# Fifteen products of 64x64 blocks in place of eighteen: g, phi and theta of blocks 2 to 8 by one scheme

## The chip, the cores and the metric

The kernel runs on one core of one Trainium2 chip. Its metric is device time in microseconds (us) of one execution. The median of three runs of the kernel before is 2480.83 us (2480.46 to 2481.8).

## The reference, cut to what matters

x has 4 images of 128 channels and 96 x 96 pixels, all in float32. Two layers of the same form, with weights of their own, are applied to it one after the other:

```python
g_x     = maxpool2(conv1x1(x, g_w, g_b))       # 128 -> 64 channels, 48 x 48 = 2304 keys
theta_x = conv1x1(x, theta_w, theta_b)         # 128 -> 64 channels, 9216 queries
phi_x   = maxpool2(conv1x1(x, phi_w, phi_b))
f    = einsum('bqc,bck->bqk', theta_x, phi_x)
attn = softmax(f, axis=-1)
y    = einsum('bqk,bkc->bqc', attn, g_x)
x    = batchnorm(conv1x1(y, W_w, W_b)) + x
```

Image and layer make eight blocks of work. A 1x1 convolution is a matrix product over the channels: g, phi and theta are three 64 x 128 matrices that meet the same x.

## The kernel before, in words

`shifted_blocks` computes everything; `general_blocks` is a second form that runs only when a flag says that sums of exponentials left their limits.

**Blocks, pairs, steps.** The order of the eight blocks is `ORDER`, which alternates images so that a block's x is finished in time. A block has 9 pairs; a pair is 1024 queries. The 2304 keys are 18 tiles of 128, taken two at a time, so a pair takes 9 steps, and a cycle of 18 steps takes an even and an odd pair. All 648 steps are one loop over `t`; `s` is `t` modulo 18, and `q` is the even pair's number.

**A step on TensorE.** The array is used as four independent 64x64 tiles. A step issues the scores of its first key tile (four products of 64 x 64 by 512 columns, `scores`, line 607), then whatever extra group the step has (`first`), then the scores of the second tile, then a second extra (`second`), then the value products of the two tiles of the step before (`values`, line 629). I call four products side by side a group. ScalarE takes `exp` of each score tile from one of two PSUM buffers (`ps_sc`, line 612). VectorE adds up the exponentials (`add_up`, lines 619 and 621); `take`, the eviction of the extra group, stands between the two add_ups of a step, or behind them. After that come the steps that were put off with `later(t, ...)`.

**What hangs on fixed steps of a cycle.** `folds` turn and add the sums of exponentials by transfers (SP and POOL queues) and DVE's `turn` at s = 15 and s = 24; `normalise` at s = 1 and 11; the projection `multiply` (line 780) at s = 3 and 13, evicted by ScalarE and added to x by an adding transfer (`add`, line 795); `put` stores a finished pair of layer 2.

**Keys and values of the next block.** While a block's pairs run, units prepare the next block's g and phi (class `Unit`). The first block makes its own (`pooled`, `chunks`). A unit covers 1536 pixels, two groups of 768; six units make a block. Its four steps (`first` to `fourth`, `UNITS`) use seven products of 64x64 blocks where the plain form takes eight, with sums of x in `sums` made by plain and adding transfers (`build`, `BUILDS`, line 434), and combined weights in `mixed`. Each step fills the two banks of `ps_misc`, which thetas, W and units share. DVE combines the products in `stage` (lines 479 to 513), pools them (517), computes the centre of phi (`centring`, lines 528 and 529), and transposes g into `gT` (559). ScalarE writes phi minus the centre in two arrangements (`spread`, lines 545, 548 and 552). Of these, `pool(1)` and `centring` are put one step after `fourth`, and `spread` a step later (`AFTER`).

**Theta.** Thetas of two pairs are made by `thetas`: two groups of 512 columns in two steps that follow each other, at s = 5 and 6 (6 and 7 in the first cycle), evicted by ScalarE (line 601). The last pair's is made alone (`theta_alone`).

**The second layer's weights** are turned and combined by DVE and ScalarE in small pieces at s = 1 and 17 of the first cycles (`late_steps`).

Of the kernel before, what the change touches and what calls it, by code (L numbers as in the profile page):

```python
# [16 lines left out]
P = 128  # L17
# [20 lines left out]
UR = 16  # L38
NU = H // UR
UN = 4 * W  # L40
UK = UN // 4
UB = 2 * UK // 32
TB = NKT // 2
UNITS = ((15, 16, 18, 20), (25, 26, 28, 30))
BUILDS = ((10, 11, 12, 12, 15), (18, 19, 20, 20, 22))
STORE = 3
AFTER = ((1, 1, 2, 4, 5), (1, 2, 2, 3, 4))
THETAS = (6, 5)
# [5 lines left out]
NORM, PROJECT = (1, 11), (3, 13)  # L54
SQ = 32
# [9 lines left out]
def shifted_blocks(ctx: ExitStack, tc: tile.TileContext, x: bass.AP, layers, out: bass.AP, flag):  # L65
# [53 lines left out]
    stage = const.tile([P, NK], F32, name="stage")  # L119
    sums = [const.tile([P, 2, UN], F32, name=f"sums_{i}") for i in range(2)]  # L120
# [40 lines left out]
    class Layer:  # L161
# [40 lines left out]
        def steps_mixed(self):  # L202

            low, high = slice(0, CI), slice(CI, P)
            g, phi = slice(0, CI), slice(CI, 2 * CI)
            m = self.mixed = const.tile([P, 3, CI], F32, name=f"mixed_{self.l}")
            w = self.gphi

            def crossed():
                nc.scalar.copy(m[low, 1, :], w[high, phi])  # L210
                nc.scalar.copy(m[high, 2, :], w[low, g])
                nc.scalar.copy(m[high, 1, :], w[low, phi])

            def combined():
                nc.vector.tensor_sub(m[low, 0, :], w[low, phi], m[low, 1, :])
                nc.vector.tensor_sub(m[high, 0, :], m[high, 1, :], w[high, phi])
                nc.vector.tensor_sub(m[high, 0, :], m[high, 0, :], m[high, 2, :])
                nc.vector.tensor_sub(m[high, 1, :], m[high, 2, :], m[high, 1, :])
                nc.vector.tensor_add(m[high, 2, :], w[high, g], m[high, 0, :])

            def copied():
                nc.scalar.copy(m[low, 2, :], m[high, 0, :])

            return [crossed, combined, copied]
# [63 lines left out]
    class Block:  # L288
# [6 lines left out]
        def begin_keys(self):  # L295
            name = self.name
            self.phi = kvp.tile([P, NK], F32, tag="phi", name=f"phi_{name}")
            self.gT = kvp.tile([P, NKT, CI], F32, tag="gT", name=f"gT_{name}")
            self.centre = kvp.tile([P, 1], F32, tag="centre", name=f"centre_{name}")

# [114 lines left out]
    class Unit:  # L415


        def __init__(self, blk, u):
            self.blk, self.u, self.name = blk, u, f"{blk.name}_{u}"
            self.s = stage[:, : 4 * UN].rearrange("p (i n) -> p i n", i=4)  # L420
            self.keys = stage[:, 4 * UN : 4 * UN + 4 * UK]
            self.half = stage[:CI, 4 * UN + 4 * UK :].rearrange("p (c n) -> p c n", c=2)

        def pixels(self, i, rows):
            some = self.blk.xt[rows, ts(self.u, UR * W)]
            return some.rearrange("p (c i n) -> p c i n", c=2, i=2)[:, :, i, :]

        def build(self):

            low, high = slice(0, CI), slice(CI, P)  # L430
            one, two = sums

            def add(dst, src):
                nc.gpsimd.dma_start(out=dst, in_=src, accum_op=ALU.add)  # L434

            def load():
                nc.sync.dma_start(out=one, in_=self.pixels(0, slice(0, P)))
                nc.sync.dma_start(out=two[high], in_=self.pixels(1, low))
                nc.sync.dma_start(out=self.half, in_=self.pixels(1, low)[:, :, UN // 2 :])

            def load_rest():
                nc.sync.dma_start(out=two[low], in_=self.pixels(1, high))

            def add_one():
                add(one[high], self.pixels(0, low))
                add(one[low], self.pixels(1, low))

            def add_two():
                add(self.half, one[high, :, UN // 2 :])
                add(two[high], one[high])  # L450

            return load, add_one, load_rest, add_two, lambda: add(two[low], two[high])

        def both(self, *some):
            for c in range(2):
                for bank, lhsT, rhs in some:
                    nc.tensor.matmul(  # L457
                        bank[ts(c, CI), :UN], lhsT=lhsT, rhs=rhs[:, c, :], start=True, stop=True
                    )

# [7 lines left out]
        def first(self):  # L468
            self.pss = two_banks(f"unit_ps_{self.name}")
            self.A, self.B = (ps[:, :UN] for ps in self.pss)  # L470
            low, high, w = slice(0, CI), slice(CI, P), self.blk.w.gphi
            self.both(
                (self.pss[0], w[low, :CI], self.pixels(1, low)),
                (self.pss[1], w[high, :CI], self.pixels(1, high)),
# [3 lines left out]
        def first_sum(self):  # L478
            nc.vector.tensor_add(self.s[:, 1, :], self.s[:, 0, :], self.B)

        def second(self):
            self.part(self.blk.w.mixed[CI:, 0, :], sums[1][CI:, :, : UN // 2], 0)

        def second_rest(self):
            self.part(self.blk.w.mixed[:CI, 2, :], self.half, 1)

        def second_sum(self):
            for i in range(2):
                dst, cols = self.s[:, 0, ts(i, UN // 2)], ts(i, UN // 2)
                nc.vector.tensor_add(dst, dst, self.pss[i][:, cols])  # L490

        def third(self):
            m = self.blk.w.mixed
            self.both(
                (self.pss[0], m[CI:, 1, :], sums[0][CI:]),
                (self.pss[1], m[:CI, 0, :], sums[0][:CI]),
            )

        def third_sum(self):
            nc.vector.tensor_add(self.s[:, 3, :], self.s[:, 0, :], self.A)  # L500
            nc.vector.tensor_sub(self.s[:, 2, :], self.B, self.s[:, 3, :])
            nc.vector.tensor_sub(self.s[:, 0, :], self.B, self.s[:, 0, :])

        def fourth(self):
            m = self.blk.w.mixed
            self.both(
                (self.pss[0], m[:CI, 1, :], sums[1][:CI]),
                (self.pss[1], m[CI:, 2, :], self.pixels(0, slice(CI, P))),
            )

        def fourth_sum(self):
            nc.vector.tensor_add(self.s[:, 3, :], self.s[:, 3, :], self.A)
            nc.vector.tensor_add(self.s[:, 0, :], self.s[:, 0, :], self.B)

        def pool(self, i):

            nc.vector.tensor_reduce(  # L517
                self.keys[:, ts(i, 2 * UK)].rearrange("p (h w) -> p h w", w=W // 2),
                self.s[:, ts(i, 2), :].rearrange(
                    "p i (h a w b) -> p (i h) w a b", a=2, b=2, w=W // 2  # L520
                ),
# [3 lines left out]

        def centring(self):
            centre = self.blk.centre
            nc.vector.tensor_reduce(centre[:CI, :], self.keys[:CI, 2 * UK :], AX.X, ALU.add)
            nc.vector.tensor_scalar(
                centre[:CI, :], centre[:CI, :], -1.0 / (2 * UK), None, ALU.mult  # L530
            )

        def parts(self):

            b = self.u * UB
            while b < (self.u + 1) * UB:
                n = min((self.u + 1) * UB, (b // TB + 1) * TB) - b
                yield b - self.u * UB, n, b // TB, b % TB
                b += n

        def spread(self):
            src = self.keys[:, 2 * UK :].rearrange("p (b k) -> p b k", k=32)
            planes = self.blk.planes().rearrange("p i (t k) -> p i t k", k=KT)
            if self.u == 0:
                nc.scalar.copy(self.blk.centre[CI:, :], self.blk.centre[:CI, :])
            for m, n, k, t in self.parts():
                dst = planes[:, :, t : t + n, ts(k, 32)]
                nc.scalar.activation(
                    dst[:, 0], src[:, m : m + n, :], AF.Identity, bias=self.blk.centre
                )  # L550
                for h in range(2):
                    nc.scalar.copy(dst[ts(1 - h, CI), 1], dst[ts(h, CI), 0])

        def square(self, side):
            src = self.keys[ts(side, CI), : 2 * UK].rearrange("p (b k) -> p b k", k=32)
            for m, n, k, t in self.parts():
                t += side * TB
                for c in range(CI // 32):
                    nc.vector.transpose(  # L559
                        self.blk.gT[ts(k, 32), t : t + n, ts(c, 32)],  # L560
                        src[ts(c, 32), m : m + n, :],
                    )

    class Pair:
# [7 lines left out]

        def theta(self, ps):
            for h in range(2):
                nc.tensor.matmul(
                    ps[ts(h, CI), :], lhsT=self.blk.w.theta,
                    rhs=self.blk.xt[:, ts(2 * self.p + h, QT)], start=True, stop=True,
                )

        def theta_alone(self):  # L580

            pss = two_banks(f"theta_ps_{self.name}")

            def make():
                for c in range(2):
                    for r in range(2):
                        nc.tensor.matmul(
# [804 lines left out]
```

## Time and profile before

| | |
|---|---|
| median of 3 runs | 2480.83 us |
| the profiled execution | 2480.92 us, span 2479.1 us, granted clock 0.999 |
| PE busy | 2468.9 us (100%) |
| DVE busy | 1974.8 us (80%) |
| ACT busy | 1670.1 us (67%) |
| POOL busy | 660.6 us (27%) |
| DMA, mean | 99 GB/s, 245.27 MB |
| queue q0 (transfers issued by POOL) | 119.78 MB, 34.7% of 16 engines |
| queue q1 (issued by SP) | 121.66 MB, 17.5% |

The span runs from the first to the last instruction that the profiler recorded; the execution is 1.8 us longer. Busy is the union of an engine's instructions. PE is TensorE, PEld its weight loads, DVE VectorE, ACT ScalarE, POOL GpSimd and SP SyncE. A name such as L621 is a line of the kernel, and `sum<-sum,exp` says what is written and from what. In the timeline a row has start, length, engine, line, operation and a count, and in brackets the idle time before it and what ended it. In the list of waits a row has total us, number of waits and the longest.

### The profile page before, as it was taken

The page shows a single profiled execution, that of the slowest core. Times are in us where ns is not written, and L with a number is a line of the kernel's source. Part 1 is how long each engine was busy: PE and PEld are TensorE (multiplying, and loading weights), DVE is VectorE, ACT ScalarE, POOL GpSimd, SP SyncE. Part 2 cuts the span into 40 slices and gives each one's busy share as a digit, 9 for nine tenths or more (in the row PEclk, how much of TensorE's full clock was granted, in tenths as well). Part 3 has the DMA queues.
Part 4 walks back from the last instruction along what each step waited for, and adds up shares of the span by engine and source line. Part 5 has one row for each costly group of instructions (what it writes and reads, how often), then busy time and mean ns, then how long its engine had stood idle before and what let it go on. Part 6 is the DMA issues. An engine that isn't in the chain of part 4 may idle for free.

```text
span 2479.1 us, 57705 instructions
## 1 busy us (share of the span) xinstructions
PE 2468.9 (100%) x23391; PEld 1145.3 (46%) x23391; DVE 1974.8 (80%) x2458; ACT 1670.1 (67%) x1836; POOL 660.6 (27%) x776
## 2 busy tenths in 40 slices
PE   9999999999999999999999999999999999999998
PEld 5444444444444444444444444444444444444443
DVE  7888878887778887888777887788876888766777
ACT  6666666666666666766666676666666666666665
POOL 0333132322133322232222332322222223222210
PEclk9999999999999999999999999999999999999999
DMA  4666465643456736575345664655435556344433
GB/s 165 104 114 133 86 121 97 114 81 60 72 104 118 134 76 118 113 132 114 70 78 110 117 118 78 130 101 98 82 61 88 109 112 113 75 78 78 78 70 61
DMA packets 151170, 245.27 MB, mean 99 GB/s; under 512 B 30310, under 2 KB 92400, under 8 KB 150896
## 3 DMA queue, kind: packets, MB, share of 16 engines
q0 software_dynamic: 69664, 119.78, 34.7%
q1 hardware_dynamic: 81064, 121.66, 17.5%
q8 instruction: 185, 3.03, 0.5%
q14 instruction: 89, 0.73, 0.1%
q10 hardware_dynamic: 168, 0.07, 0.0%
HBM read 37.56 MB, written 19.16 MB: 23 GB/s over the span
## 4 chain that ended last, share of the span: by engine, by line
PE 98%; DVE 1%; DMA 0%; issue 0%; ACT 0%; SPq 0%; DVEq 0%; ACTq 0%
PE sc L607 45%; PE av L629 44%; PE W_ps L780 2%; PE theta_ps L284 2%; PE unit_ps L457 2%; PE unit_ps L463 1%; PE gphi_ps L336 0%; DVE sum L621 0%; PE gphi_ps L284 0%; DMA x<-in_x_dram 0%; DVE sum L654 0%; ACT exp L612 0%; DVE gT L559 0%; DMA turned<-sum 0%; DVE x L839 0%
## 5 line engine op out<-in xcount | busy, mean ns | idle before, releaser
L612 ACT ACTIVATE exp<-sc,nshift 128x1024 f32<-128x1024 f32 x1296 | 1397.0, 1113 | 741.1 <-PE sc L607 734.8
L621 DVE TENSOR_TENSOR sum<-sum,exp 128x1024 f32<-128x1024 f32 x1151 | 1409.0, 1224 | 397.0 <-ACT exp L612 344.3
L607 PE MATMUL sc<-theta,phi 64*64 64x512 f32 x10368 | 1572.3, 589 | 0.4 <-ACT exp L612 0.4
L629 PE MATMUL av<-exp,gT 64*64 64x512 f32 x10368 | 1468.0, 589 | 0.0
L607 PEld LDWEIGHTS sc<-theta,phi 64*64 64x64 f32 x10368 | 582.4, 133 | 598.9 <-issue 568.4
L629 PEld LDWEIGHTS av<-exp,gT 64*64 64x64 f32 x10368 | 555.4, 133 | 595.6 <-issue 571.6
L685 POOL DMA_DIRECT2D turned<-sum x140 | 114.9, 946 | 1270.7 <-DMA turned<-sum 818.0
L698 POOL DMA_DIRECT2D sum<-turned x280 | 253.5, 1593 | 74.6 <-DMA sum<-turned 71.8
L619 DVE TENSOR_TENSOR sum<-exp,exp 128x1024 f32<-128x1024 f32 x72 | 88.1, 1223 | 64.7 <-ACT exp L612 64.6
L795 POOL DMA_DIRECT2D x<-halves x70 | 88.2, 1260 | 189.4 <-ACT halves L791 188.4
L434 POOL DMA_DIRECT2D sums<-x x84 | 94.8, 1463 | 69.1 <-DMA sums<-x 43.8
L434 POOL DMA_DIRECT2D sums<-sums x84 | 100.6, 1198 | 8.1 <-PE sc L607 3.7
L769 POOL DMA_DIRECT2D halves<-halves x70 | 100.2, 1431 | 0.4 <-issue 0.4
L457 PE MATMUL unit_ps<-sums,mixed 64*64 64x384 f32 x504 | 100.1, 482 | 0.0
L780 PE MATMUL W_ps<-halves,WT 64*64 64x512 f32 x568 | 99.7, 590 | 0.1
L284 PE MATMUL theta_ps<-x,thetaT 64*64 64x512 f32 x560 | 98.9, 589 | 0.0
L636 ACT COPY halves<-av 128x1024 f32<-128x1024 f32 x71 | 71.9, 1012 | 35.4 <-PE av L629 35.4
L791 ACT ACTIVATE halves<-W_ps,shift 128x512 f32<-128x512 f32 x140 | 88.8, 692 | 0.3 <-PE W_ps L780 0.3
L434 POOL DMA_DIRECT2D stage<-sums x42 | 39.6, 942 | 178.1 <-DMA sums<-x 178.1
L517 DVE TENSOR_REDUCE stage<-stage 128x192 f32<-128x768 f32 x84 | 78.2, 945 | 0.0
L559 DVE STREAM_TRANSPOSE gT<-stage 32x192 f32<-32x192 f32 (+1 forms) x224 | 71.5, 319 | 4.1
L457 PE MATMUL unit_ps<-x,gphiT 64*64 64x384 f32 x336 | 50.3, 482 | 0.0
(122 smaller groups left out, 830.6 us busy)
## 6 DMA issues: line engine op xcount, KB each, us to landing
x<-halves POOLq DMA_DIRECT2D x70, 512.0 KB, 5.4
turned<-sum SPq DMA_DIRECT2D x140, 128.0 KB
turned<-sum POOLq DMA_DIRECT2D x140, 128.0 KB, 4.6
halves<-halves POOLq DMA_DIRECT2D x70, 256.0 KB, 6.6
halves<-row SPq DMA_DIRECT2D x140, 128.0 KB
out_dram<-x SPq DMA_DIRECT2D x35, 512.0 KB
sums<-x SPq DMA_DIRECT2D x42, 384.0 KB
sums<-x SPq DMA_DIRECT2D x84, 192.0 KB
```

Of the source, the lines that this page charges most:

```text
L284: nc.tensor.matmul(out, lhsT=lhsT, rhs=rhs, start=step == 0, stop=step == 1)
L434: nc.gpsimd.dma_start(out=dst, in_=src, accum_op=ALU.add)
L457: nc.tensor.matmul(bank[ts(c, CI), :UN], lhsT=lhsT, rhs=rhs[:, c, :], start=True, stop=True)
L607: nc.tensor.matmul(ps[ts(c, CI), ts(h, QT)], lhsT=self.blk.keys_of(k, c, h), rhs=self.th[ts(h, CI), :], start=True, stop=True,)
L612: nc.scalar.activation(e, ps, AF.Exp, bias=nshift)
L621: nc.vector.tensor_add(self.sum, self.sum, e)
L629: nc.tensor.matmul(self.av[ts(h, CI), ts(r, QT)], lhsT=self.blk.gT[ts(r, CI), k, :], rhs=e[ts(r, CI), ts(h, QT)], start=(k == 0), stop=(k ...
L685: nc.gpsimd.dma_start(out=self.turned[ts(h, CI)], in_=self.sum[ts(h, CI), ts(h, QT)], accum_op=ALU.add,)
L698: nc.gpsimd.dma_start(out=folded()[ts(i, SQ)], in_=self.turned[ts(i, SQ), ts(k, n)], accum_op=ALU.add,)
L769: nc.gpsimd.dma_start(out=self.y, in_=self.halves[:, QT:], accum_op=ALU.add)
L780: nc.tensor.matmul(self.pss[h][ts(c, CI), :], lhsT=self.blk.w.W[ts(h, CI), ts(c, CI)], rhs=self.y[ts(h, CI), :], start=True, stop=True,)
L791: nc.scalar.activation(self.halves[:, ts(h, QT)], self.pss[h], AF.Identity, bias=self.blk.w.shift,)
```

## The change

For blocks 2 to 8 one scheme makes g, phi and theta of three groups of 384 x 2 pixels from fifteen 64x64 block products for eighteen. A unit now covers 2304 pixels (384 columns at each of three places in both halves of the image), four units make a block, one per cycle, and each has eight steps (`STEPS`), of which seven have four products of 384 columns and one four of 192. Ten adding transfers and five loads per unit make the sums of x. Biased theta leaves DVE through `put_theta` into a DRAM buffer, and `load_theta` brings a pair's part back. A pair of these blocks is two runs of 512 pixels, one in each half of the image, instead of 1024 pixels in a row (`runs`). Block 1 makes theta as before, always at s = 6 and 7. `centring` is called inside `spread`. The pieces of layer 2's weights move to s = 1, 4 and 10.

```diff
-UNITS = ((15, 16, 18, 20), (25, 26, 28, 30))
-BUILDS = ((10, 11, 12, 12, 15), (18, 19, 20, 20, 22))
-AFTER = ((1, 1, 2, 4, 5), (1, 2, 2, 3, 4))
-THETAS = (6, 5)
+STEPS = (8, 9, 11, 12, 14, 17, 20, 23)
+THETAS = 6
+LOADS = (4, 12)
+PREPARE = (1, 4, 10)
...
+            def lower():
+                sub(m[low, 1, :], w[low, g], w[low, phi])
+                ...
+                nc.scalar.copy(m[high, 6, :], m[low, 6, :])
+
+            def upper():
+                sub(m[high, 0, :], w[high, g], m[high, 1, :])
+                nc.scalar.copy(m[low, 0, :], m[high, 0, :])
+                ...
+            return [crossed, lower, upper, rest]
...
+            return [
+                (2, load(of(two, high), x(0, low))),
+                (3, load(lambda: self.half, lambda: self.pixels(0, high)[:, :, UN // 2 :])),
+                (4, add(of(two, high), x(1, low))),
+                (5, load(of(one, low), x(0, low))),
+                (5, load(of(one, high), x(1, low))),
+                (6, add(of(one, low), x(0, high))),
+                (8, add(of(one, high), of(one, low))),
+                (10, load(of(two, high), x(0, low))),
+                (11, add(of(one, low), x(2, low))),
+                (11, add(of(one, high), x(1, high))),
+                (13, add(of(two, high), x(2, low))),
+                (14, add(of(one, low), x(2, high))),
+                (14, add(of(one, high), x(2, high))),
+                (17, add(of(one, low), x(1, high))),
+                (20, add(of(one, low), x(1, low))),
+            ]
...
+        def second(self):
+            low, high = slice(0, CI), slice(CI, P)
+            self.both(
+                (self.mixed(low, 1), self.pixels(1, low)), (self.mixed(high, 2), sums[1][high])
+            )
+            nc.scalar.copy(self.s[:, 4, :], self.A)
...
+        def third_sum(self):
+            nc.vector.tensor_add(self.s[:, 5, :], self.s[:, 5, :], self.A)
+            nc.vector.tensor_sub(self.s[:, 2, :], self.s[:, 1, :], self.B)
+            nc.vector.tensor_add(self.s[:, 3, :], self.s[:, 3, :], self.s[:, 2, :])
...
+        def eighth_sum(self):
+            nc.vector.tensor_sub(self.s[:, 4, :], self.s[:, 4, :], self.A)
+            nc.vector.tensor_sub(self.s[:, 0, :], self.s[:, 0, :], self.A)
             nc.vector.tensor_add(self.s[:, 0, :], self.s[:, 0, :], self.B)
+            self.put_theta(1, 4)
+
+        def put_theta(self, j, i):
+            nc.sync.dma_start(out=self.blk.thetas[:, self.columns(j)], in_=self.s[:, i, :])
...
+        def pools(self):
+            return [
+                (11, lambda: self.pool(0, 0, 5)), (13, lambda: self.pool(1, 0, 3)),
+                (16, lambda: self.pool(1, 1, 3)), (18, lambda: self.pool(0, 1, 2)),
+                (19, lambda: self.pool(0, 2, 5)), (23, lambda: self.pool(1, 2, 0)),
+                (21, lambda: self.square(0)), (22, lambda: self.square(1)),
+                (24, self.spread),
+            ]
...
         def spread(self):
...
             if self.u == 0:
+                self.centring()
                 nc.scalar.copy(self.blk.centre[CI:, :], self.blk.centre[:CI, :])
...
+        def load_theta(self):
+            self.th = work.tile([P, QT], F32, tag="theta", name=f"theta_{self.name}", bufs=3)
+            nc.sync.dma_start(out=self.th, in_=self.blk.thetas[:, ts(self.p, QT)])
...
+        first = (n - 1) * NP * NB // CYCLE * CYCLE
+        later(first, lambda n=n: set_x(n))
+        later(first + STEPS[3], lambda n=n: begin(n))
         for u in range(NU):
-            ...
+            unit, cycle = Unit(blocks[n], u), first + u * CYCLE
+            for i, t in enumerate(STEPS):
+                assert cycle + t not in stages
+                stages[cycle + t] = (unit, i)
+            for i, step in unit.build() + unit.pools():
+                later(cycle + i, step)
```

## The prediction

> **What bounds the kernel now.** I read the page first, then TensorE's waits, then the timeline of single steps.
>
> ```profile
> PE 2468.9 (100%) x23391; PEld 1145.3 (46%) x23391; DVE 1974.8 (80%) x2458; ACT 1670.1 (67%) x1836; POOL 660.6 (27%) x776
> ...
> PE 98%; DVE 1%; DMA 0%; issue 0%; ACT 0%; SPq 0%; DVEq 0%; ACTq 0%
> ```
>
> TensorE is busy from end to end and carries 98% of the chain that ended last. A busy PE need not be PE at its peak, so I ask what it waits for:
>
> ```profile
> PE warm_ps L893 <- POOL ident masks.py:199: 1.4, 1, 1.4
> PE gphi_ps L336 <- DMA x<-in_x_dram: 0.7, 1, 0.7
> PE sc L607 <- ACT exp L612: 0.4, 1, 0.4
> PE good_ps L1079 <- DVE good L1077: 0.3, 1, 0.3
> ```
>
> That is 2.8 us in all: any column taken off PE shortens the run, and any wait put in front of PE lengthens it. What a column costs stands in the timeline of PE, where each score row opens a step:
>
> ```profile
> 795.08 2.26 PE L607 MATMUL sc<-theta,phi 64*64 64x512 f32 x16
> ...
> 799.37 1.40 PE L607 MATMUL sc<-theta,phi 64*64 64x512 f32 x8
> ...
> 803.45 1.45 PE L607 MATMUL sc<-theta,phi 64*64 64x512 f32 x9
> ...
> 807.20 2.26 PE L607 MATMUL sc<-theta,phi 64*64 64x512 f32 x16
> ...
> 810.64 1.40 PE L607 MATMUL sc<-theta,phi 64*64 64x512 f32 x8
> ```
>
> The last stretch, 810.64 - 807.20 = 3.43 us, is a plain step: two score and two value groups, each of four 64x64 products side by side over 512 columns, so 0.858 a group. The first has a theta group more (4.29 = 3.43 + 0.86), the second a unit group of 384 columns (4.08 = 3.43 + 0.645), the third one of 192 (3.75 = 3.43 + 0.32). Cost is proportional to columns.
>
> **What the skill says.** The Trainium skill, "TensorEngine Tiling (Array Packing)", Instruction Overhead, puts some 60 cycles on each matmul, which would punish many narrow products. Here 384 columns cost 0.645/0.858 = 0.75 of 512, exactly their share; the forecast goes by the trace. "PSUM — Partial Sum Buffer", Engine vs sequencer instructions, says that the queues of ScalarE and VectorE are strict FIFO. The trace agrees: in the stretch below, the exp at 722.71 starts only when ScalarE has finished the four small instructions before it, though its score group began at 721.03 and an exp otherwise starts about 1.5 us after that (717.60 to 719.12 in the step before). The forecast rests on this one.
>
> **PE: what is removed and added.** Removed: 42 units of three groups of 384 and one of 192 (3 x 0.645 + 0.32 = 2.26), 94.7 us, and 63 theta groups (blocks 2 to 8), 54.1. Added: 28 units of seven groups of 384 and one of 192 (4.83), 135.3. Net 13.5 us less. If nothing waits, the profiled run of 2480.9 becomes 2467.4.
>
> **Throughput of the others.** DVE: 19 operations of 384 columns per unit (0.55 to 0.61 each, rows L500 to L513 and L799) are some 299 us for 141 now; pools and transposes stay about even. Busy goes from 1975 to about 2130, 86%. ACT loses 63 evictions of theta at 0.69 and gains copies: some 25 us less. POOL issues 10 adds per cycle of 18 steps, as now (two units of 5). SP issues 8 per unit plus two theta loads a cycle, at about 0.6 each, for 8 loads now; its theta stores wait for their own step's DVE sums. None becomes the bound. So the price lies in order: who waits inside a step.
>
> **The wait that I charge: centring.** Now the centre is computed (L528, L529) one step before `spread` reads it:
>
> ```profile
> 719.12 2.12 ACT L612 ACTIVATE exp<-sc,nshift 128x1024 f32<-128x1024 f32 x2 [1.01 <-PE sc L607]
> ...
> 719.42 0.35 DVE L528 TENSOR_REDUCE centre<-stage 64x1 f32<-64x192 f32 x1
> 719.81 0.15 DVE L529 TENSOR_SCALAR centre<-centre 64x1 f32<-64x1 f32 x1
> ...
> 721.26 0.19 ACT L545 COPY centre<-centre 64x1 f32<-64x1 f32 x1
> 721.48 0.45 ACT L548 ACTIVATE phi<-stage,centre 128x192 f32<-128x192 f32 x1
> ...
> 721.97 0.71 ACT L552 COPY phi<-phi 64x192 f32<-64x192 f32 x2
> 722.71 1.11 ACT L612 ACTIVATE exp<-sc,nshift 128x1024 f32<-128x1024 f32 x1
> ```
>
> The centre is ready at 719.96, ACT takes it at 721.26 without waiting, and the next exp is some 0.2 late. After the change `centring` is called inside `spread`, at step 24 of a unit (s = 6 of the next cycle): DVE does it after both add_ups of that step, and ACT's copy of the centre waits behind its exps, with all later exps queued behind it.
>
> DVE's clock, from starts in the timeline: the first add_up starts 2.67 into a step; add to add 1.33, add to another operation 1.14; 384-column operations 0.47 apart, 0.65 if one reads the last one's result; a transpose of 288 columns about 0.48 (269 ns at 96, 369 at 192).
> - Step 4: 2.67 + 1.33 + 1.14 + two transposes (about 1.05) = 6.2, so 2.8 into step 5.
> - Step 5 (`eighth_sum`): add 1.14, sums 0.47 + 0.65 + 0.47, add 1.14, pool 0.47: free at 7.1, which is 3.05 into step 6 (step 5 is 4.08 long).
> - Step 6: two adds, 5.5; reduction (0.35 at 192 columns, about 0.45 at 288) and scaling 0.15: the centre is there at 6.15.
> - ACT starts its copy at 6.2. From it to the next exp is 1.45 above; three of the four are half as wide again, at 0.08 each: 1.7. The first exp of step 7 starts 7.9 into step 6, 4.45 into step 7, instead of 1.46.
> - It ends at 5.55; with about 0.1 from semaphore to product, step 8's first score group, which needs that exp's PSUM buffer (`ps_sc` has two), starts at 5.65 for 3.43.
>
> So PE stands still for 2.2 us, once in each of blocks 3 to 8: 13.2. With DVE on time in step 6 it is 1.85, with DVE 0.5 later 2.7 (11 to 16 in all). In block 2 the theta groups of steps 6 and 7 lengthen both by 0.86 and leave about 0.5.
>
> **Waits in block 1.** Its thetas now go to s = 6 in all its cycles (they stood at s = 5 in all but the first), one step after `eighth`, and both use the two banks of `ps_misc`. The last reader, third in `eighth_sum`, ends at 5.05 + 0.55 = 5.6 into step 5; theta wants the bank at 4.08 + 0.86 = 4.94. Layer 2's weight steps, now at s = 1, 4 and 10, put 0.85 of transposes (four of 0.2), and once five small differences (1.2), ahead of it at s = 4: waits of 1.6, 1.6 and 1.9, 5.0 together; with no lag carried over, 2.2.
> In the first cycle `upper` makes ACT wait, at t = 5, for a difference that DVE reaches after two pools, two adds and eight transposes (3.0): some 9.4 into the step, against 5.75 when the next exp is due; 1.3 of that is slack, so about 2.4. The kernel before has a wait of 0.6 of this sort at 171 (W behind sums), which may go.
>
> **Costed at nothing.** Bank by bank: `third` (step 11) to `fourth` (12): the second bank's reader ends at 4.83, the product is due at 4.95; `fourth` to W (13): reader ends at 5.7, due 5.8, after DVE's pool and normalise. Each has about 0.1 to spare; if it is gone, 28 x 0.1 to 0.3, up to 8. `split` to `second` (8 to 9): ACT's two copies end at 4.1, due 4.6. W to `fifth` (13 to 14): evictions end at 4.75, due 5.15. The start of x's second half is needed earlier by the first unit; the page moves 165 GB/s in the first slice, 10 MB in 62 us, so it is there.
> The adds: `fifth` needs two that may start when `third` is done, 2.1 into step 11; 11.2 us remain. Such a pair, with the queue empty, landed 3.8 and 5.6 after issue, and 10.0 at worst among 84. For `sixth` 9.7 us remain, for `seventh` and `eighth` as much or more, with one add each. `third` needs load, add, add: 17.5 us from the load's issue, for about 3 (estimate: the shortest add) + 3.8 to 5.2 + 4.5 to 6.8. Theta's load has five steps. Covered, by 2 us or more.
>
> **Sum.** -13.5 + 13.2 + 0.5 + 5.0 + 2.4 - 0.6 + 0.5 (small waits) = +7.5 on the profiled 2480.9, of which 2479.1 is the span; the median is 0.1 lower: 2488.3.
>
> **Rivals.**
> - Faster, the other side: the wait on the centre is absorbed. For that ACT must take the centre by 3.95 into step 6 rather than 6.2, so that step 7's first exp ends by 3.3. It speaks for it that DVE idles 397 us before add_up, so it may not lag; against it that even without lag the centre comes at 5.75, and that FIFO leaves ACT no way round. Then -13.5 + 2 to 6: about 2471.
> - Much slower: the adding transfers come late. For: longer chains through POOL, landings up to 10.0. Against: the slack above. If each unit waits 1.5 us: 28 x 1.5 = 42 more, about 2530; it decides from landings beyond 9.7.
> - The change does not do what it says: narrow products cost more than their columns. The steps of 4.08 and 3.75 exclude it nearly.
>
> **Chances.** My forecast 0.67 (its own range 2481 to 2497), absorbed 0.17, late transfers 0.13, the last 0.03. A measurement of this kernel can tell about 0.2%, 5.0 us. In the forecast's case a quarter lies within that. Faster 0.17, same 0.20, slower 0.63. The range takes in the absorbed case's middle and the lighter end of late transfers: 2471 to 2508.
>
> **What would show it.** The list of PE's waits names sc waiting for exp, at six places of about 2 us, one in each of blocks 3 to 8; ACT's waits name the copy of the centre waiting for DVE, 2 us and more; theta_ps waits for DVE three times in the first 300 us. PE's unit rows add to 28 x 4.83. It is wrong if the sc row stays at 0.4, or if unit_ps waits for DMA.

## The result, and the profile after

The changed kernel takes 2489.95 us (median of 7 runs, 2488.32 to 2490.93) for 2481.11 us before in the same comparison: 1.0034 of it, with a 95% interval of 1.0023 to 1.0046, so slower by 8.8 us. The profiled execution took 2488.51 us. The page, with the chain of work that ended last:

```profile
span 2486.7 us, 58096 instructions
...
PE 2461.7 (99%) x23335; PEld 1464.3 (59%) x23335; DVE 2064.1 (83%) x2639; ACT 1643.3 (66%) x1789; POOL 755.5 (30%) x846
...
PE 93%; DVE 4%; ACT 2%; issue 1%; DMA 0%; SPq 0%; DVEq 0%; ACTq 0%
```

TensorE's busy time fell by 7.2 us while the span grew by 7.6: it now stands still. The chain says at whose hands. It goes through VectorE (4%) and ScalarE (2%) where it held 98% TensorE, and transfers have no part in it. TensorE's waits (total, times, longest):

```profile
PE sc L684 <- ACT exp L689: 12.4, 9, 2.1
PE theta_ps L295 <- DVE stage L599: 2.2, 3, 1.2
...
PE unit_ps L498 <- ACT theta L678: 0.5, 1, 0.5
```

and ScalarE's:

```profile
ACT centre L637 <- DVE centre L628: 17.3, 7, 2.6
...
ACT mixed L221 <- DVE mixed L219: 5.4, 2, 3.2
ACT mixed L225 <- DVE mixed L224: 5.3, 2, 3.4
```

The two lists belong together. A score group never waits for ScalarE's speed (it is 66% busy); it waits for an exp that stands in ScalarE's queue behind a copy whose source VectorE has not made yet. The timeline shows one of the places, while the third block's pairs run and the centre of the next block is made (start, duration, engine, line, what; in brackets the idle time before it and who ended it):

```profile
739.15 2.02 PE L684 MATMUL sc<-theta,phi 64*64 64x512 f32 x16
...
740.39 2.12 ACT L689 ACTIVATE exp<-sc,nshift 128x1024 f32<-128x1024 f32 x2 [1.45 <-PE sc L684]
...
741.52 0.55 DVE L608 TENSOR_REDUCE pooled<-stage 128x96 f32<-128x384 f32 x1
741.98 2.55 DVE L698 TENSOR_TENSOR sum<-sum,exp 128x1024 f32<-128x1024 f32 x2
742.58 2.02 PE L684 MATMUL sc<-theta,phi 64*64 64x512 f32 x16
...
744.44 0.44 DVE L627 TENSOR_REDUCE centre<-pooled 64x1 f32<-64x288 f32 x1
744.91 0.15 DVE L628 TENSOR_SCALAR centre<-centre 64x1 f32<-64x1 f32 x1
745.10 0.19 ACT L637 COPY centre<-centre 64x1 f32<-64x1 f32 x1 [2.58 <-DVE centre L628]
...
746.78 2.12 ACT L689 ACTIVATE exp<-sc,nshift 128x1024 f32<-128x1024 f32 x2
...
747.95 1.09 PE L684 MATMUL sc<-theta,phi 64*64 64x512 f32 x8 [1.62 <-ACT exp L689]
```

Three score rows open three steps: 742.58 - 739.15 = 3.43, a plain step, and 747.95 - 742.58 = 5.37. The second is 1.94 too long. ScalarE was free at 742.51 and the score group of 742.58 was there for an exp from about 743.8 (740.39 - 739.15 = 1.24 after its start, as in the step before); that exp starts at 746.78, because ScalarE had stopped at the copy of the centre. VectorE had all it needed for the centre at 742.07, when the pool ended, but took both add_ups first.

The same subtraction can be made for every step: its length less its columns at 0.858 us for 512. In the kernel before this leaves 1.0 and 0.4 us at two steps with W, and else nothing over 0.25 once the first three steps are past. In the changed kernel it leaves 1.9 to 2.0 in each of blocks 3 to 8, and some stalls in the first five cycles; every other step is of its exact length to within 0.1, but for two with 0.3 and 0.14 and one with -0.2. At a few steps three records of value products stand on the far side of a step's border, so a single figure can be 0.3 off; over a longer stretch this cancels. The table under "Why the prediction came right" adds them up.

### The profile page after: what moved, and what is told of

Read it like the earlier page. It is cut to its first block, busy times and chain, and to the rows that moved or that the text cites. A ratio compares the mean times of both kernels' runs of the same rounds, so it can differ in the third digit from the quotient of the medians.

```text
span 2486.7 us, 58096 instructions
## 1 busy us (share of the span) xinstructions
PE 2461.7 (99%) x23335; PEld 1464.3 (59%) x23335; DVE 2064.1 (83%) x2639; ACT 1643.3 (66%) x1789; POOL 755.5 (30%) x846
## 4 chain that ended last, share of the span: by engine, by line
PE 93%; DVE 4%; ACT 2%; issue 1%; DMA 0%; SPq 0%; DVEq 0%; ACTq 0%
PE sc L684 43%; PE av L706 42%; PE unit_ps L489 5%; DVE sum L698 3%; PE W_ps L857 2%; ACT exp L689 1%; PE gphi_ps L349 0%; PE unit_ps L498 0%; PE theta_ps L295 0%; ACT phi L641 0%; DVE gT L646 0%; DVE stage L599 0%; DVE stage L598 0%; DMA x<-in_x_dram 0%; ACT phi L639 0%
## 5 line engine op out<-in xcount | busy, mean ns | idle before, releaser
L684 PE MATMUL sc<-theta,phi 64*64 64x512 f32 x10368 | 1387.3, 590 | 12.4 <-ACT exp L689 12.4
L706 PE MATMUL av<-exp,gT 64*64 64x512 f32 x10368 | 1315.8, 589 | 0.0
L706 PEld LDWEIGHTS av<-exp,gT 64*64 64x64 f32 x10368 | 653.8, 133 | 450.6 <-issue 226.5
L684 PEld LDWEIGHTS sc<-theta,phi 64*64 64x64 f32 x10368 | 660.8, 133 | 426.9 <-issue 199.9
L458 POOL DMA_DIRECT2D sums<-x x252 | 292.6, 1409 | 482.6 <-PE unit_ps L489 304.7
L608 DVE TENSOR_REDUCE pooled<-stage 128x96 f32<-128x384 f32 x168 | 91.6, 545 | 0.0
L489 PEld LDWEIGHTS unit_ps<-sums,mixed 64*64 64x64 f32 x896 | 61.3, 133 | 39.6 <-issue 16.1
L489 PE MATMUL unit_ps<-x,mixed 64*64 64x384 f32 x448 | 74.3, 483 | 0.0
L646 DVE STREAM_TRANSPOSE gT<-pooled 32x288 f32<-32x288 f32 x112 | 52.5, 469 | 2.2
L851 DVE TENSOR_TENSOR halves<-halves 128x512 f32<-128x512 f32 x71 | 48.6, 684 | 0.0
```

What stands on the lines that cost most here:

```text
L458: return lambda: nc.gpsimd.dma_start(out=dst(), in_=src(), accum_op=ALU.add)
L489: nc.tensor.matmul(bank[ts(c, CI), :UN], lhsT=lhsT, rhs=rhs[:, c, :], start=True, stop=True)
L608: nc.vector.tensor_reduce(pooled[:, side, ts(j, UK)].rearrange("p (h w) -> p h w", w=W // 2), self.s[:, i, :].rearrange("p (h a w b) -> p ...
L684: nc.tensor.matmul(ps[ts(c, CI), ts(h, QT)], lhsT=self.blk.keys_of(k, c, h), rhs=self.th[ts(h, CI), :], start=True, stop=True,)
L706: nc.tensor.matmul(self.av[ts(h, CI), ts(r, QT)], lhsT=self.blk.gT[ts(r, CI), k, :], rhs=e[ts(r, CI), ts(h, QT)], start=(k == 0), stop=(k ...
```

## Experiments

Each was compared with the kernel before in its own runs. The changed kernel stands 8.8 us above it; the differences below are from there. Their line numbers lie up to 6 away from those of the changed kernel (in the one built on the kernel before, 1 away from that kernel's).

**The centre a step sooner.**

```diff
-                (24, self.spread),
+                (23, self.centre_first), (24, self.spread),
...
+        def centre_first(self):
+            if self.u == 0:
+                self.centring()
+
         def spread(self):
...
             if self.u == 0:
-                self.centring()
                 nc.scalar.copy(self.blk.centre[CI:, :], self.blk.centre[:CI, :])
```

> The centre is computed at the end of step 23 of a unit (s = 5 of the next cycle, behind the pool that it needs), and spread only copies it. Theory (ScalarE's FIFO: the copy of the centre waits for VectorE, and the exps queue behind it): in the trace of after, the centre then comes at about 742.6 in the third block instead of 745.1, when ScalarE has just ended its exps; the next exp is some 0.3 us late, which 1.3 us of slack take. All seven stalls go: six of 1.9 and about 1.1 in block 2, 12.8 us in all, 2477 us. Rival (ScalarE's extra 0.25 us of copies in spread, or VectorE's lag from the sums of the eighth product, is what makes the exps late): at least half of each stall stays, 2483 us or more.

Measured: 2477.59 us, 0.9984 of the kernel before (0.9977 to 0.9990), so 3.7 us under it and 12.6 under the changed kernel. The timeline in the third block:

```profile
735.97 2.24 PE L687 MATMUL sc<-theta,phi 64*64 64x512 f32 x16
...
739.40 2.25 PE L687 MATMUL sc<-theta,phi 64*64 64x512 f32 x16
739.61 0.14 DVE L628 TENSOR_SCALAR centre<-centre 64x1 f32<-64x1 f32 x1
739.68 2.54 DVE L701 TENSOR_TENSOR sum<-sum,exp 128x1024 f32<-128x1024 f32 x2
739.78 0.19 ACT L640 COPY centre<-centre 64x1 f32<-64x1 f32 x1 [0.25 <-DVE centre L628]
...
742.84 1.45 PE L687 MATMUL sc<-theta,phi 64*64 64x512 f32 x9
```

The copy of the centre starts 3.81 us into the step instead of 5.95, the next step is 3.44 long, and over all blocks the lost 12.8 us of this kind have shrunk to 0.3. It is the order of the centre and the add_ups on VectorE that cost them, not ScalarE's wider copies, which are unchanged. The prediction's limit for this, 3.95 us, was met by 0.14 and held.

**ScalarE's copies of the weight differences a step later.**

```diff
             def lower():
...
-                nc.scalar.copy(m[high, 6, :], m[low, 6, :])
             def upper():
+                nc.scalar.copy(m[high, 6, :], m[low, 6, :])
                 sub(m[high, 0, :], w[high, g], m[high, 1, :])
-                nc.scalar.copy(m[low, 0, :], m[high, 0, :])
...
             def rest():
+                nc.scalar.copy(m[low, 0, :], m[high, 0, :])
```

> ScalarE's copies of the weight differences in lower and upper are issued one step of that preparation later than VectorE's differences. Theory (the same kind of wait: ScalarE stands at a copy whose source VectorE has not made): the stall of 3.3 us in the first cycle goes, and of the fourth cycle's stalls 1.4 us at s = 5 and 6 and 0.65 at s = 12: about 5 us, 2485 us. Rival (the first cycle is bound by VectorE's amount of work, eight transposes and two pools beside the differences): 1 us at most.

Measured: 2483.86 us, 1.0011 (1.0004 to 1.0017), 6.3 us under the changed kernel. The 3.5 us of the first cycle are gone, the two stalls of 0.8 and 0.65 in the fourth cycle too, and of ScalarE's waits for mixed (10.7 us) one of 0.8 is left. Those stalls add up to 4.9 us; the profiled executions lie 4.5 apart (2488.51 and 2484.05). The last section says where the remaining 1.8 of the median may come from.

**The eighth product's sums before the add_ups.**

```diff
+        if stage_of == 7:
+            take()
+            take = None
         for i in range(KB):
             if t < total:
                 pairs[now].add_up(j * KB + i)
```

> The sums that read the eighth product's two banks run before both add_ups of their step, in all 28 units. Theory (block 1's thetas wait for the bank that these sums hold): the banks come free some 1.5 us sooner, the stalls of 1.2 and 1.0 us at s = 6 of the second and third cycles go, and about 0.5 to 1 us of the fourth cycle's; 2.2 to 3.2 us, 2487.2 us. The add_ups that come later in 25 other places cost nothing, as VectorE idles there. Rival (add_up's delay holds back the exp buffers or the next step's sums): 2490 us or more.

Measured: 2488.11 us, 1.0031 (1.0019 to 1.0043): 2.1 us less, somewhat below the range expected. The theta_ps row has left TensorE's waits, and the steps with theta are too long by less than 0.1 in all for 4.0 before: the bank was the cause. But the centring stalls grew: by 0.2 to 0.5 in each of blocks 3 to 8, and by 1.0 in block 2, whose theta stall had stood in the same step as its centre and had given VectorE the time for it. The expectation that the move costs nothing elsewhere was wrong while a late centre follows one step behind.

**The three together**, and the second layer's weight pieces of s = 4 at s = 7 (`PREPARE = (1, 7, 10)`).

> The three edits together, and the second layer's weight pieces of s = 4 at s = 7. Theory (the change takes 13.5 us of columns off TensorE, and what it lost was waits of these three kinds alone): TensorE's stalls shrink from 20.6 us above those of the kernel before to 1 us or less, 2468 to 2470 us, some 12 us under the kernel before. Rival (narrow products cost more than their columns, or the stalls move elsewhere): 2475 us or more.

Measured: 2467.62 us, 0.9945 (0.9931 to 0.9959): 13.7 us under the kernel before, 22.5 under the changed one. TensorE's waits are again those of the kernel before:

```profile
PE warm_ps L975 <- POOL ident masks.py:199: 1.4, 1, 1.4
PE sc L687 <- ACT exp L692: 0.4, 1, 0.4
PE gphi_ps L349 <- DMA x<-in_x_dram: 0.3, 1, 0.3
PE good_ps L1155 <- DVE good L1153: 0.3, 1, 0.3
```

This also settles what the products cost. The columns counted from the traces at 0.858 us for 512 are 13.5 us fewer than before, and 13.7 is what the medians show once the waits are out (13.2 between the profiled executions): seven groups of 384 and one of 192 have no price beyond their columns. It is the best of the kernels run here.

**The kernel before, with its centre called in spread.** One part of the change alone, on the old scheme.

```diff
-            if u == 0:
-                later(when[0], unit.centring)
...
             if self.u == 0:
+                self.centring()
                 nc.scalar.copy(self.blk.centre[CI:, :], self.blk.centre[:CI, :])
```

> The kernel before, with one part of the change alone: centring is called inside spread, a step later. Theory by the clock of its trace: VectorE reaches the centre after both add_ups, at about 722.85 instead of 719.42, ScalarE's copy starts at 723.4 instead of 721.26, and the exp behind it is 2.1 us later. The theta group of that step and the slack of 1.3 us take all but 0.2 to 0.5 us of it: 1.4 to 3.5 us over seven blocks, 2483.5 us. Rival (any centre that comes late costs its 1.9 us, whatever else the step holds): 13 us, 2494 us. Rival (all of it is absorbed): 2481 us.

Measured: 2484.07 us, 1.0012 (1.0005 to 1.0018), 2.8 us more. Lists of waits:

```profile
ACT centre L546 <- DVE centre L529: 14.3, 7, 2.1
...
PE sc L608 <- ACT exp L613: 0.4, 1, 0.4
```

ScalarE waits some 2.0 us seven times, for 2.5 in the changed kernel, and TensorE's list doesn't even show it: the steps are longer by 0.4 to 0.8 in each block. The theta group that still stands in the step gives the exp 0.86 us more time. The exp behind the copies is also less late, in the third block 725.72 - 722.16 = 3.56 us into its step:

```profile
722.16 1.26 PE L608 MATMUL sc<-theta,phi 64*64 64x512 f32 x8
...
725.72 2.12 ACT L613 ACTIVATE exp<-sc,nshift 128x1024 f32<-128x1024 f32 x2
```

In the changed kernel it is 746.78 - 742.58 = 4.20: there the copy of the centre comes 0.4 later in the step, and the copies last 0.2 longer. The two parts, 0.86 and 0.64, make up the difference of 1.5 between this step's stall (0.43) and the changed kernel's (1.94). So the scheme itself made the late centre dear: for the larger part by taking theta off TensorE, and with it the cover.

**The adding transfers later.** Two of the transfers that the fifth product reads are made to wait for VectorE; nothing else is edited, but what stands behind them in POOL's queue waits with them.

```diff
+            def touch():
+                nc.vector.tensor_copy(one[:, 0, :1], one[:, 0, :1])
...
+                (11, touch),
                 (11, add(of(one, low), x(2, low))),
                 (11, add(of(one, high), x(1, high))),
```

> The two adding transfers that the fifth product reads start only when VectorE has copied one column of their tile in place, behind the sums of step 11: some 4 us later than now, in all 28 units. Theory (the prediction's slack of 11.2 us against landings of 5.6, 10.0 at worst): 7 us are left, so nearly nothing waits, 0 to 10 us more, 2490 to 2500 us. Rival (these transfers are near the path already): 28 x 2 us or more, 2545 us.

> The same behind the sums of step 12: the transfers have about 3 us before the fifth product is due. Theory: the first lands 0.8 us late and the second 2.6 us or more, so TensorE waits 2.6 to 4 us in each of 28 units, 70 to 110 us more, about 2580 us; the row of unit_ps waiting for DMA appears with 28 places. Rival (the transfers never decide, since their data is taken in another order): no change.

Measured: 2517.96 us, 1.0154 (1.0138 to 1.0169), and 2676.72 us, 1.0786 (1.0769 to 1.0802): 27.9 and 186.6 us above the changed kernel, 1.0 and 6.7 in each unit. Both are above what was expected. TensorE's waits in the first and in the second:

```profile
PE unit_ps L493 <- DMA sums<-x: 9.4, 20, 1.4
```

```profile
PE unit_ps L493 <- DMA sums<-x: 98.2, 56, 3.1
```

From the trace, in us after the start of step 11 (medians of 28 units):

| kernel | first add issued, landed | second issued, landed | fifth product's last part |
|---|---|---|---|
| changed | 2.1, 6.5 | 2.7, 9.3 | 13.8 |
| behind the sums of step 11 | 7.7, 12.0 | 8.3, 14.3 | 14.8 |
| behind the sums of step 12 | 11.4, 15.6 | 12.0, 18.0 | 18.7 |

The landing takes the same 4.2 to 6.6 us wherever it starts, so the expectation was out by the start: VectorE is through with step 11 only 5.6 us later than the add starts now, not 4. From 14.3 on the transfers decide, as the much slower rival had it; as written they land 4.0 us before the fifth product is due at 13.3, and 0.5 before it in the worst of the 28 units. Of the 6.7 us in the last row the transfer explains 18.7 - 13.8 = 4.9. For the rest see the last section.

**The same kernel again**, the one with the centre a step sooner, for two more profiled executions.

> The kernel with the centre a step before, unchanged, for another profiled execution: its times lie in two groups, near 2475.8 and near 2478.0 us. Theory: in the slower group TensorE's clock is halved behind the 2.1 us stall of the first cycle (as in the trace of the kernel with the eighth product's sums first, where 16 products behind that stall took 3.6 us for 2.1), so an execution near 2478.0 shows a granted clock near 0.5 for some 3 us after 50 us, and one near 2475.8 shows 1.0 there. Rival: the 2.2 us come from somewhere else, and the clock stays at 1.0 in both.

> As the run before it: another profiled execution of the same kernel, for the group that the first did not fall in.

Measured: 2477.77 and 2476.44 us. TensorE's busy time and clock (PEclk, the column before the last two) just behind the first cycle's stall, in the slower one:

```profile
49.00:50.00 1.00, 0.00 (x0) 1.00 0.00 0
50.00:51.00 1.00, 0.81 (x4) 0.65 0.00 0
51.00:52.00 1.00, 1.00 (x12) 0.50 0.00 0
52.00:53.00 1.00, 1.00 (x12) 0.50 0.00 0
53.00:54.00 1.00, 1.00 (x8) 0.65 0.00 0
54.00:56.00 2.00, 2.00 (x24) 1.00 0.00 0
```

and in the other:

```profile
50.00:51.00 1.00, 0.41 (x4) 1.00 0.00 0
51.00:52.00 1.00, 1.00 (x12) 1.00 0.00 0
```

The step behind the stall is 1.75 us too long in the first and 0.2 in the second. But for one of 0.4 us in the second, all other steps agree within 0.2 us. So what sets the slower execution apart is the halved clock, as the theory had it.

## Why the prediction came right

2488.3 us was predicted; 2489.95 was measured, and 2488.51 in the profiled execution, against which the sum of 2488.4 was made. That the median lies 1.4 above the profiled execution was not foreseen; the last section has a likely cause. That the sum came out to 0.1 us is luck: its terms are off by up to 1.5 us, in both directions, and cancel. By its terms, in us, the measured ones from lengths of steps (the last row but one holds what is left of the 7.6):

| term | predicted | measured |
|---|---|---|
| columns off TensorE | -13.5 | -13.5 |
| centring, blocks 3 to 8 | 13.2 | 11.7 |
| centring, block 2 | 0.5 | 1.1 |
| thetas of block 1 | 5.0 | 4.8 |
| `upper` in the first cycle | 2.4 | 3.5 |
| old waits of W (1.45 gone; 0.45 new at two other steps) | -0.6 | -1.0 |
| small | 0.5 | 1.0 |
| sum | 7.5 | 7.6 |

- *Columns.* Held to 0.1 us, and the kernel with all three edits turned it into time.
- *Centring.* The mechanism and the six places are as predicted, and moving the centre removes them. The copy of the centre came 5.95 us into the step, predicted 6.2, and the stall is 1.95 instead of 2.2: VectorE's lag at the start of step 6 was sized too large. The add_ups started 2.83 into it, where 2.67 is on time and a lag until 3.05 had been worked out. "With DVE on time 1.85" was the nearer value. In block 2 the wait on the centre leaves 0.3 us; the other 0.8 is in the next step, where a unit's product waits for ScalarE's two evictions of theta, which stand behind the late exps (the `unit_ps` row above). The prediction had left that out; both go when the centre is made a step sooner.
- *FIFO.* The rule of the Trainium skill, "PSUM — Partial Sum Buffer", Engine vs sequencer instructions, that ScalarE's queue is strict FIFO, carried the forecast. The trace agrees: an exp that could start at about 743.8 started at 746.78, 1.68 us after the copy in front of it.
- *Thetas.* As the table has it, 4.8 for 5.0, but not by the same parts. The first two stalls are 1.2 and 1.0 for 1.6 each, the third is 1.8 for 1.9 (each known to 0.3 only), with another 0.8 in the step ahead of it, which is not the bank but an exp behind the copy in `lower`. Two errors cancel here: the carried lag was too large, and the copy of the second layer was not seen. Another 0.65 us in the fourth cycle, `upper` of the second layer, went the same way and stands under "small".
- *First cycle.* 3.5 for 2.4. The step that failed is that `upper` was priced with `lower` costing nothing: ScalarE waited for `lower`'s copy too (one of the two waits at L221), so that the first exp of the next step began at 40.88, 2.38 us into a step that starts at 38.50, for 1.24 in the undisturbed step of the timeline above. The add_ups behind it and then `upper` were 0.9 later, and its copy came at 48.84, 10.3 into the step for 9.4 worked out.
- *Costed at nothing.* Right, with margins as thin as 0.1: the bank hand-overs from `third` to `fourth` and from `fourth` to W lengthen no step. The transfers' cover is real but thinner than stated, 4.0 us in the median instead of 5.6 (11.2 - 5.6), since the later of the two is issued 0.6 after the first and lands 6.6 after that.
- *VectorE's throughput.* 2064 us for a forecast of 2130; the direction held, and it is not the bound. The sums that go were taken at 141 us, without a row of 29, and sums that follow each other start 0.47 us apart though each lasts 0.55, so that their durations add up to more than their busy time. ScalarE has 26.8 us less for 25.

Of the rivals, "absorbed" is out for the kernel as written and is what the first experiment made of it. "Late transfers" decides only when they start over 4 us later. "Narrow products dear" is out.

## What to carry to other kernels

When one engine bounds a kernel, its saved columns are worth their full price only if nothing small stands between two other engines inside a step: count for each copy in a FIFO queue when its source is made, and put the producer one step ahead of it. Work that is taken off the bounding engine also takes away the time that covered a late neighbour, so redo the slack of the steps that got shorter. Then look at the order within the step: the edits that won 22.5 us moved some ten lines and removed no work.

## What the hardware showed that was not expected

TensorE's granted clock can halve behind a short stall. Behind the same 2.1 us of waiting in the first cycle it was 1.0 in two of three executions of one kernel; in the third it was 0.5 for 3.41 us, and the step then lasted 1.6 us longer. The executions of the kernels that keep this stall spread over 2.6 to 3.1 us (the changed kernel, the one with the centre sooner, the one with the eighth's sums first) and, with later transfers and so more waits, over 6.7 and 7.5; those of the kernels without it spread over 1.4 (copies a step later) and 2.0 (all three edits). That can account for most of the 1.4 us by which the changed kernel's median lies above its profiled execution (three of its seven executions took 2488.32 to 2488.87, four 2489.95 to 2490.93), and so for the 1.8 us that taking the stall away won in the median beyond the profiled executions; for the changed kernel this is argued, as only the kernel with the centre sooner was profiled in both forms.

In the kernel with the transfers behind step 12 it goes with the fifth product: two waits with two matmul records between them, and then

```profile
913.00:914.00 1.00, 0.83 (x2) 0.19 (x2) 0.76 (x1) 0.00 (x0) 1.00 (x4) 1.00 1.09 102
914.00:915.00 1.00, 0.00 (x0) 0.00 (x0) 0.00 (x0) 0.00 (x0) 1.00 (x2) 1.00 0.93 108
...
916.00:917.00 1.00, 1.00 (x12) 0.69 (x8) 0.38 (x1) 0.00 (x0) 0.32 (x2) 0.54 1.12 195
917.00:918.00 1.00, 1.00 (x9) 0.60 (x5) 1.00 (x3) 0.00 (x0) 1.00 (x2) 0.50 1.09 180
```

(the columns are the busy times of PE, PEld, DVE, ACT and POOL, then PEclk, share and rate of DMA). All 28 units of that kernel have such a stretch at 0.5: 14 of them 3.41 us long, where the unit loses 6.2 us in the mean, and 14 of them 6.83 us, where it loses 7.3. Against the 4.9 of the transfers this is the rest of the 6.7; its mean clock is 0.972, where the others have 0.998 or 0.999.

The Trainium skill, "TensorE: Matmul & The Clock Gate", What's actually happening, describes a gate that halves the clock after an idle window of about 3.4 us, on windows that run freely. The traces agree on the windows. All changes to 0.5 in one trace lie on a grid of 3.413 us, to within 4 ns (29 of them over 2587 us in the kernel with the transfers behind step 12), and the grid lies differently in each execution. But the window before the change need not be idle throughout. Length, busy time of PE and clock, window by window, in the execution of the kernel with the centre sooner that took 2477.77 us, then in the changed kernel's (its grid is taken from the drop at the end of its trace):

```profile
46.89:50.30 3.41, 1.29 (x15) 1.00 0.00 0
50.30:53.71 3.41, 3.41 (x20) 0.50 0.00 0
```

```profile
46.64:50.05 3.41, 1.52 (x15) 1.00 0.00 0
50.05:53.46 3.41, 3.19 (x28) 1.00 0.00 0
```

In the first the whole stall falls into one window, which is idle for 2.12 us, and the next window has half the clock. In the second a border cuts the same stall, no window is idle for more than 1.89, and the clock stays. The other executions with this stall fit: 2.11 us in one window and a halved clock in the kernel with the eighth's sums first, at most 1.93, 1.66, 1.19 and 1.19 and a full clock in four others. The centring stalls never put more than 1.81 us into one window, and never halved it. So it is luck, from one execution to the next, whether a stall of 2.1 us costs 1.6 us more. The limit is not sharp, or TensorE's idle time is not all that counts: behind the two waits of the fifth product windows with 1.6 to 1.95 us of idle time were followed by either clock. What exactly decides there stays open.
